# A graph kernel's edge messages: rows spread by three bf16 products instead of one in fp32

## The chip, the cores and the metric

The kernel runs on one core of a Trainium2 chip. The metric is the device time of one execution in microseconds (us). The core has five engines that run their own instruction streams and wait for each other by semaphores: TensorE (PE; its weight loads are shown as PEld), VectorE (DVE), ScalarE (ACT), GpSimd (POOL) and SyncE (SP, which only issues DMAs here). Sixteen DMA engines serve all queues.

## The reference, cut to what matters

Two graph layers on 32768 nodes of width 256 and 524288 edges that are sorted by target. Layer 0 is attention within blocks of 128 nodes; layer 1 passes messages along the edges in both directions:

```python
h = jnp.maximum(_layernorm(x, axis=-1), 0.0)
x = x + _L0_gnn_ref(h, ...)                      # attention in blocks of 128 nodes
h = jnp.maximum(_layernorm(x, axis=-1), 0.0)     # "h1" in the kernel
# layer 1, _L1_gnn_ref (h is batch-normalised first)
a_in = jax.ops.segment_sum(feat_in[src] * iw[:, None], dst, num_segments=N)
a_out = jax.ops.segment_sum(feat_out[dst] * ow[:, None], src, num_segments=N)
# then gates (sigmoid, tanh) on a_in, a_out and h
```

The change concerns `a_out`: each edge takes the row of its target node `dst`, times a weight, and adds it to the row of its source node `src`. The kernel does the weight matrices afterwards, so what is moved along the edges is `h1` itself, in fp32.

## The kernel before

Work comes in this order: sorting and tables (to about 1000 us), then the stage that the change touches (to about 9000 us), then adding up the messages by target and by source (to about 15100 us), then the gates.

In the touched stage two things are woven together by hand.

*Attention groups.* `group(g)` handles 512 nodes (four blocks of 128). It does not emit code but fills `todo`, a list of functions by step: `@at(t)` puts one at step t. A block b has its attention at steps from B = 17 + 11 b: scores (`sc`), their maxima (`nm`, VectorE), exponentials (`pr`, ScalarE), their transposes (`pt`, TensorE) and the copy of these (`PT`), the products with the values, `o`, the output product `y`, then `x1g` (VectorE) and its row statistics. At b = 2 (B = 39) and b = 3 (B = 50) the second layer norm follows: `std` at B + 17, `nmr` on VectorE at B + 18, the row `h1g` on ScalarE at B + 18 + n, its transpose on TensorE at B + 19 + n (into `pt` for block 1, into `sc` for the others; each of these has one buffer), its copy `h1T` on ScalarE at B + 20 + n. Blocks 0 to 2 are done together at b = 2 (n = 0 to 2, steps 57 to 61), block 3 at b = 3 (steps 68 to 70). `x1_d`, `h1_d` and `h1T_d` are the results' copies in DRAM. `h1_d` is read twice: by the spreading described next, and by the later stage that adds up by target.

*Spreading.* `spread(k, lo, hi)` takes a third of the edges (k = 0, 1, 2) in items of 128 edges whose targets lie in one block of 128 nodes. `turns` runs 64 items to a turn, 4352 items in 68 turns, and mostly four turns to a loop round. The first 63 turns each carry one attention group: the group's step u is emitted at step 64 r + u of turn r, behind the items' own work. An item i passes through `steps` at fixed distances: `fetch` (SP loads the 128 rows of the target block as `hb`, 10 buffers) at t = i, `spread_lanes` at i + 4, `select` at i + 6 (`selT`, four items at a time: a 0/1 matrix of which row each edge takes; and `oh`, which source block each edge goes to), `rank` (three bf16 products into `R`), `product` (`mp` = `selT` times `hb`, two buffers) and `place` (`jk`, on VectorE) at i + 8, `scale` (ScalarE writes `mp` times the edge's weight to `msg`) and `scatter` (POOL sends the messages to their places in `msg_d`) at i + 9. So at step t TensorE ranks and multiplies item t - 8. All engines but POOL run in the order written here:

```python
steps = ((0, fetch), (4, spread_lanes), (6, select), (8, rank), (8, product), (8, place), (9, scale), (9, scatter))
```

In each step the items' parts are emitted first, then `for f in todo.get(t, ()): f()`, the group's functions in the order in which `group` put them there: those of an earlier block ahead of those of a later one.

Of the kernel before, what the change touches and what calls it, by code (L numbers as in the profile page):

```python
# [11 lines left out]
F32 = mybir.dt.float32  # L12
# [7 lines left out]
P = 128  # L20
H = 8
DH = 32
D = H * DH
KC = D // P
HC = H // KC
GB = 4
# [122 lines left out]
BF16 = mybir.dt.bfloat16  # L149
NB = 256  # L150
T1 = 128
# [348 lines left out]
def gnn_kernel(ctx, tc, x, src, dst, edge_attr, edge_type, w_in_e, w_out_e,  # L500
               Wq, bq, Wk, bk, Wv, bv, Wo, bo, gate_table, We, be,
               gamma, beta, W_in, b_in, W_out, b_out, W_x2i, b_x2i, W_h2h, out):
    nc = tc.nc
    N = x.shape[0]
# [4 lines left out]
    dram = ctx.enter_context(tc.tile_pool(name="dram", bufs=1, space=DRAM))  # L509
# [33 lines left out]
    x1_d = dram.tile([N, D], F32, name="x1_d")  # L543
    h1T_d = dram.tile([D, N], F32, name="h1T_d")
    h1_d = dram.tile([N, D], F32, name="h1_d")
    rec_d = dram.tile([E + T2, 4], F32, name="rec_d")
    ends = [sum(PH[:k + 1]) for k in range(len(PH))]
    assert ends[-1] == E
# [11 lines left out]

    x1_g = x1_d.rearrange("(g b p) d -> g p b d", b=GB, p=P)
    h1_g = h1_d.rearrange("(g b p) d -> g p b d", b=GB, p=P)
    h1T_g = h1T_d.rearrange("(c p) (g n) -> g p c n", p=P, n=GN)


# [15 lines left out]
    for k, (lo, hi) in enumerate(edges):  # L581
# [5 lines left out]
        at = lambda t, f: t[rs, f, 0:CS]  # L587
        of = lambda f, i: tabr_d[rs, i:i + CT, f].rearrange("c (a i) -> c a i", i=4)[:, :, 1:4]
        _, _, r = item_tables(tc, cpool, cn, f"o{k}", scnt[k], 0, T3, CS, 1, NCO[k], hi - lo, [
            ("first", of(0, 0)), ("to", of(1, LAG)),  # L590
            ("keep", at(tabb_d, 1)), ("node", at(tabb_d, 2))])
# [20 lines left out]
    def numbers(ap, most):  # L612


        return [v.with_bounds(max_val=m) for v, m in zip(nc.values_load_multi_w_load_instructions(
            ap, engines=(mybir.EngineType.SP,), min_val=0, max_val=int(OUT),
            skip_runtime_bounds_check_because="bounded in item_tables")[1], most)]
# [21 lines left out]
    with tc.tile_pool(name="ld", bufs=1) as lp:  # L639
# [4 lines left out]
        for k in range(K):  # L644
            n, node = NC1[k], itp[k][1]
# [15 lines left out]
        g = lp.tile([P, 1], F32, name="g")  # L661
        nc.vector.tensor_copy(g, lead)
        for k in range(K):
            left = lp.tile([P, 1], F32, name="left")
            nc.vector.tensor_scalar(left, g, -1.0, float(NG), op0=ALU.mult, op1=ALU.add)
            at = lambda i: slice(i * K + k, i * K + k + 1)
# [20 lines left out]
    with ExitStack() as c1:  # L687

        ap = c1.enter_context(tc.tile_pool(name="a_1", bufs=1))
# [23 lines left out]
        xg, xb, x1g, h1g = (ap.tile([P, GB, D], F32, name=n) for n in ("xg", "xb", "x1g", "h1g"))  # L713
        hT, qT, h1T = (ap.tile([P, KC, GN], F32, name=n) for n in ("hT", "qT", "h1T"))
        nmr = ap.tile([P, GB], F32, name="nmr")

        mv, rstd = ([ap.tile([P, GB] + w, F32, name=f"{n}{i}") for i in range(2)] for n, w in (("mv", [2]), ("rstd", [])))

        def group(g, bias=None):
# [3 lines left out]
            def at(t):  # L723
                def put(f):
                    todo.setdefault(t, []).append(f)
                return put
# [9 lines left out]
            def transposed(name, rows):  # L736
                tp = a_ps.tile([P, KC, P], F32, name=name)
                for k in range(KC):
                    nc.tensor.transpose(tp[:, k], rows[:, k * P:(k + 1) * P], ident)
                return tp  # L740

            @at(0)
            def _():
                nc.scalar.dma_start(xg, x_g[g])
# [82 lines left out]
            for b in range(GB):  # L827
                B = 17 + 11 * b
                cols = slice(b * P, (b + 1) * P)
                s = {}  # L830
# [86 lines left out]
                for n, u in enumerate(range(bs.start, bs.stop)):  # L917
                    h = {}

                    @at(B + 18 + n)  # L920
                    def _(u=u):
                        nc.scalar.activation(h1g[:, u], x1g[:, u], AF.Relu, bias=nmr[:, u:u + 1], scale=rstd[1][:, u:u + 1])

                    @at(B + 19 + n)
                    def _(u=u, h=h):
                        h["tp"] = transposed("pt" if u == 1 else "sc", h1g[:, u])

                    @at(B + 20 + n)
                    def _(u=u, h=h):
                        nc.scalar.copy(h1T[:, :, u * P:(u + 1) * P], h["tp"])  # L930
# [4 lines left out]

            @at(B + 19)
            def _():
                nc.sync.dma_start(h1_g[g], h1g)

            @at(B + 21)  # L940
            def _():
# [8 lines left out]
        def alone(g, bias=None):  # L950
            todo = group(g, bias)
            for t in sorted(todo):
                for f in todo[t]:
                    f()
# [12 lines left out]
        sp = c1.enter_context(tc.tile_pool(name="p_s", bufs=2))  # L967
        op = c1.enter_context(tc.tile_pool(name="p_o", bufs=8))
        ip = c1.enter_context(tc.tile_pool(name="p_i", bufs=NM))
        hp = c1.enter_context(tc.tile_pool(name="p_h", bufs=10))  # L970
# [21 lines left out]
        def spread(k, lo, hi):  # L992
# [61 lines left out]
            def fetch(i, q, c, turn):  # L1054
                if q % 4 == 0:
                    c["at"] = numbers(c["row"][:, q:q + 4], [N - P] * 4)
                hb = turn["hb", i] = hp.tile([P, D], F32, name="hb")
                nc.sync.dma_start(hb, h1_d[ds(c["at"][q % 4], P)])

            def spread_lanes(i, q, c, turn):  # L1060
                if q % 4 == 0:
# [3 lines left out]

            def select(i, q, c, turn):
                if q % 4 == 0:
                    sel = turn["sel", i // 4] = sp.tile([P, 4, T1], F32, name="selT")
                    nc.vector.tensor_scalar(sel, turn["bc"], cn["lane"], None, op0=ALU.is_equal)
                oh = turn["oh", i] = op.tile([P, NB], BF16, name="oh")  # L1070
                nc.vector.tensor_scalar(oh, cn["iota1"], c["ed"][:, 0, q:q + 1], None, op0=ALU.is_equal)  # L1071

            def product(i, q, c, turn):
                mp = turn["mp", i] = pp.tile([P, D], F32, name="mp")
                nc.tensor.matmul(mp, turn["sel", i // 4][:, q % 4], turn.pop(("hb", i)), start=True, stop=True)  # L1075

            def add(what, of, to, turn):
                oh = turn["oh", of]
# [34 lines left out]


            steps = ((0, fetch), (4, spread_lanes), (6, select), (8, rank), (8, product), (8, place), (9, scale), (9, scatter))

            def turns(begin_at, end, nr, groups):

                with tc.For_i(begin_at, end, nr, hint_engines=ENGINES) as it:
                    cs, turn, todo, n = [], {}, {}, nr * CI  # L1120
                    last = steps[-1][0]
                    with tc.manual_schedule(engines=IN_ORDER):
                        for t in range(n + last):
                            r, q = divmod(t, CI)
                            if r < nr:
                                after = ds((it + (r + 1)).with_bounds(min_val=0, max_val=NC1[k]), 1)
                                if q == 0:
                                    cs.append({})
                                    begin(cs[r])
                                    if groups is not None:  # L1130
                                        for u, fs in group((it + groups + r).with_bounds(min_val=0, max_val=NG - 1)).items():
                                            assert u < CI + last
                                            todo.setdefault(t + u, []).extend(fs)
                                if q == 10:
                                    window(after)
                                if q == 24:
                                    more = derive(after)
                                if q >= 24:
                                    next(more, None)
                            for lag, step in steps:  # L1140
                                i = t - lag
                                if 0 <= i < n:
                                    step(i, i % CI, cs[i // CI], turn)
                            for f in todo.get(t, ()):
                                f()
                        add("ones_b", n - 1, n, turn)
                        add("triu", n - 2, n, turn)
                        add("triu", n - 1, n - 1, turn)
# [41 lines left out]
    with ExitStack() as c2:  # L1190
        fp = c2.enter_context(tc.tile_pool(name="q_f", bufs=1))
        wp = c2.enter_context(tc.tile_pool(name="q_w", bufs=2))
        sp = c2.enter_context(tc.tile_pool(name="q_s", bufs=4))
        mp = c2.enter_context(tc.tile_pool(name="q_m", bufs=8))
# [144 lines left out]
    with ExitStack() as c3:  # L1339
# [10 lines left out]
        with tc.For_i(0, NG // UE, 1) as it:  # L1350
            for u in range(UE):
                g = it * UE + u
# [71 lines left out]
```

## Time and profile before

| | |
|---|---|
| median of 12 runs | 17246.58 us (17218.29 to 17273.27) |
| the profiled execution | 17258.26 us, its span 17256.5 us |
| granted TensorE clock, mean | 0.913 |
| TensorE busy | 14052.0 us (81%) |
| VectorE, ScalarE, POOL busy | 58%, 39%, 54% |
| products `mp` (line L1075) | 8704 matmul instructions, two to a product |
| DMA | 2975.49 MB, 172 GB/s over the span |

In the profile a line such as L1075 is that line of the kernel file. `out<-in` names the tiles, with numbers left out of the names: `h_d` stands for `h1_d`, `x_d` for `x1_d`, `msg_d` for each of the three. A matmul's duration reaches from its start to its modelled end, and matmuls overlap; so the pace of TensorE is read from one start to the next. "[1.90 <-ACT pr L851]" behind a line of the timeline is the engine's idle time ahead of it and who ended it. A table of waits gives, for each pair of waiter and releaser, total us, times and longest. In the table by stretches the last columns are the granted clock of TensorE (1 is full speed), the DMA engines' busy share and GB/s.

### The profile page before, as it was taken

How to read it: one execution, taken by the hardware profiler on the slowest of the kernel's cores; microseconds unless marked ns; L12 is line 12 of the kernel's file. 1: busy time of each engine (PE TensorE's matmuls, PEld its weight loads, DVE VectorE, ACT ScalarE, POOL GpSimd, SP SyncE). 2: the span in 40 equal slices, each digit the busy share in tenths (PEclk: the TensorE clock that was granted, in tenths of full speed). 3: DMA queues.
4: the chain of work that ended last, by engine and by line, in shares of the span. 5: the costliest groups of instructions: out<-in, count | busy, mean ns of one | idle time of the engine just before them, and what ended most of it. 6: DMA issues, size and time to landing. Idle time of an engine off the chain costs nothing. (4 is left out here: it accounts for less than half of the span.)

```text
span 17256.5 us, 292322 instructions
## 1 busy us (share of the span) xinstructions
PE 14052.0 (81%) x71746; PEld 10243.3 (59%) x71746; DVE 10066.7 (58%) x33799; ACT 6724.1 (39%) x16865; POOL 9321.8 (54%) x9307
## 2 busy tenths in 40 slices
PE   2068888878888878888759999898888888888989
PEld 1045555555555555565547777777777777643433
DVE  8766667666766766776655555555555555422222
ACT  0034444444544444454434444444444444300000
POOL 0045555555555555555567777776767667622221
PEclk6589999989999989999879999999999999999999
DMA  1035555544554545555448888788878888843332
GB/s 64 10 119 165 165 165 164 161 150 159 168 163 159 164 127 163 167 165 162 155 155 243 243 241 243 233 240 231 236 227 237 228 236 240 197 129 106 110 117 91
DMA packets 1829630, 2975.49 MB, mean 172 GB/s; under 512 B 299498, under 2 KB 1288135, under 8 KB 1827670
## 3 DMA queue, kind: packets, MB, share of 16 engines
q1 hardware_dynamic: 1169398, 1550.90, 29.8%
q0 software_dynamic: 430768, 1160.40, 22.6%
q10 hardware_dynamic: 227888, 246.51, 4.6%
q8 instruction: 582, 9.54, 0.2%
q14 instruction: 994, 8.14, 0.2%
HBM read 2123.63 MB, written 1248.64 MB: 195 GB/s over the span
## 5 line engine op out<-in xcount | busy, mean ns | idle before, releaser
L1108 POOL DMA_INDIRECT msg_d<-msg,pi x4352 | 4298.2, 988 | 3027.8 <-ACT msg L1091 1087.7
L1230 POOL DMA_INDIRECT rows<-h_d,ixc x3584 | 3414.8, 953 | 1376.9 <-PE ps_i L1244 354.8
L1099 DVE SCALAR_TENSOR_TENSOR jk<-iota,edc,R 128x256 f32<-128x256 bf16 x4352 | 2076.4, 477 | 1914.2 <-PE R L1079 1882.4
L1091 ACT ACTIVATE msg<-mp,edc 128x256 f32<-128x256 f32 x4352 | 2064.1, 479 | 2749.5 <-PE mp L1075 2728.5
L1265 ACT ACTIVATE selo<-lane_row,sl 128x128 f32<-128x128 f32 x5040 | 1671.1, 393 | 3389.2 <-DVE sl L1262 2742.1
L1244 PE MATMUL ps_i<-rows,sel 128*128 128x257 f32 x8960 | 2504.3, 398 | 335.7 <-DVE acc L1248 259.1
L1075 PE MATMUL mp<-hb,selT 128*128 128x256 f32 x8704 | 2766.2, 401 | 8.0 <-ACT msg L1091 7.4
L1272 PE MATMUL ps_o<-m,selo 128*128 128x257 f32 x10080 | 2567.7, 392 | 216.9 <-ACT selo L1266 214.5
L1272 PEld LDWEIGHTS ps_o<-m,selo 128*128 128x128 f32 x10080 | 1868.2, 195 | 527.0 <-ACT selo L1266 166.7
L1244 PEld LDWEIGHTS ps_i<-rows,sel 128*128 128x128 f32 x8960 | 1564.8, 198 | 589.5 <-DVE acc L1248 370.6
L1237 DVE TENSOR_SCALAR sel<-lane_row,ed 128x128 f32<-128x128 f32 x4480 | 1395.4, 360 | 605.4 <-PE idle L1245 548.5
L1075 PEld LDWEIGHTS mp<-hb,selT 128*128 128x128 f32 x8704 | 1402.5, 203 | 82.9 <-ACT msg L1091 13.5
L1071 DVE TENSOR_SCALAR oh<-iota,edc 128x256 bf16<-128x256 bf16 x4352 | 1419.9, 326 | 4.1
L1079 PE MATMUL R<-oh,ones_b 128*128 128x256 bf16 x4352 | 1247.6, 287 | 119.3 <-DVE jk L1099 110.9
L1276 DVE SCALAR_TENSOR_TENSOR acc<-acc,blk,ps_o 128x257 f32<-128x257 f32 x1680 | 807.7, 481 | 835.3 <-PE ps_o L1272 700.0
L1079 PE MATMUL R<-oh,tri 128*128 128x256 bf16 x4352 | 1239.8, 285 | 0.0
L1079 PE MATMUL R<-oh,triu 128*128 128x256 bf16 x4352 | 1233.2, 284 | 0.0
L1248 DVE SCALAR_TENSOR_TENSOR acc<-acc,blk,ps_i 128x257 f32<-128x257 f32 x2240 | 1073.2, 479 | 213.9 <-DMA sin_d<-acc 97.9
L1262 DVE TENSOR_SCALAR sl<-m,blk 128x3 f32<-128x3 f32 x1680 | 426.2, 254 | 1131.9 <-DMA m<-msg_d 1117.9
L1230 POOL DMA_INDIRECT rows<-h_d,ixh x896 | 854.8, 954 | 374.8 <-issue 138.6
L1266 ACT ACTIVATE selo<-selo,one 128x384 f32<-128x384 f32 x1680 | 1035.1, 616 | 52.5
L1245 PE MATMUL idle<-lane_row,sel 128*128 128x128 f32 x4480 | 850.0, 278 | 138.0 <-DVE sel L1237 121.5
(366 smaller groups left out, 20255.4 us busy)
## 6 DMA issues: line engine op xcount, KB each, us to landing
m<-msg_d SPq DMA_DIRECT2D x1680, 396.0 KB
hb<-h_d SPq DMA_DIRECT2D x4352, 128.0 KB
sin_d<-acc SPq DMA_DIRECT2D x2240, 128.5 KB
sout_d<-acc SPq DMA_DIRECT2D x1680, 128.5 KB
msg_d<-msg,pi POOLq DMA_INDIRECT x4352
more<-sout_d ACTq DMA_DIRECT2D x128, 514.0 KB
rows<-h_d,ixc POOLq DMA_INDIRECT x3584
a<-sin_d ACTq DMA_DIRECT2D x64, 514.0 KB
```

The source lines that it names most:

```text
L1071: nc.vector.tensor_scalar(oh, cn["iota1"], c["ed"][:, 0, q:q + 1], None, op0=ALU.is_equal)
L1075: nc.tensor.matmul(mp, turn["sel", i // 4][:, q % 4], turn.pop(("hb", i)), start=True, stop=True)
L1079: nc.tensor.matmul(R[to % 2], cn[what], oh, start=False, stop=False, skip_group_check=True)
L1091: nc.scalar.activation(msg[:, q % 4, 0:D], turn.pop(("mp", i)), AF.Copy, scale=c["ed"][:, 1, q:q + 1])
L1099: nc.vector.scalar_tensor_tensor(jk, cn["iota1"], c["ed"][:, 0, q:q + 1], R[i % 2], op0=ALU.is_equal, op1=ALU.mult, accum_out=c["pf"][:, q ...
L1108: s = nc.gpsimd.indirect_dma_start(out=msg_d[k][:], out_offset=bass.IndirectOffsetOnAxis(ap=c["pi"][:, j:j + 1], axis=0), in_=msgs[i // 4 ...
L1230: nc.gpsimd.indirect_dma_start(out=rows[(2 * i + r) % NR][:, 0:D], out_offset=None, in_=h1_d[:], in_offset=bass.IndirectOffsetOnAxis(ap=(i ...
L1237: nc.vector.tensor_scalar(sel[:, r], cn["lane_row"], c["ed"][:, 0, r, i:i + 1], c["ed"][:, 1, r, i:i + 1], op0=ALU.is_equal, op1=ALU.mult)
L1244: nc.tensor.matmul(ps, sel[:, r], rows[(2 * i + r) % NR], start=(r == 0), stop=(r == 1))
L1248: nc.vector.scalar_tensor_tensor(acc[0][i % NA], acc[0][(i - 1) % NA], c["blk"][:, 0, i:i + 1], c.pop(("t_ps", i)), op0=ALU.mult, op1=ALU.add)
L1265: nc.scalar.activation(sel[:, r], cn["lane_row"], AF.Abs, bias=sl[:, r:r + 1])
L1272: nc.tensor.matmul(ps, sel[:, r], m[:, r, 0:FW], start=(r == 0), stop=(r == T3 // P - 1))
```

## The change

The rows of `h1` are also stored as three bf16 parts, whose sum is the fp32 row: the first is `h1g` rounded to bf16, the second is what is left of it, rounded, the third the rest of that. ScalarE makes the first two, VectorE takes the differences and writes the third, four blocks a group, at steps B + 19 to B + 21 (+ n). The parts go to a new DRAM tensor `h1s_d` by a DMA on SP at step B + 22; the store of `h1_d` moves from SP's queue to ScalarE's. `fetch` loads the three parts (192 KB an item in place of 128 KB), `selT` becomes bf16, and `product` multiplies it with each part in turn and adds the three up in `mp`. All else stays.

```diff
+    h1s_d = dram.tile([N, 3, D], BF16, name="h1s_d")
+    h1s_g = h1s_d.rearrange("(g b p) s d -> g p b s d", b=GB, p=P)
...
+        h1s = ap.tile([P, GB, 3, D], BF16, name="h1s")
+        rest = ap.tile([P, GB, D], F32, name="rest")
...
                     @at(B + 19 + n)
                     def _(u=u, h=h):
                         h["tp"] = transposed("pt" if u == 1 else "sc", h1g[:, u])
 
+                    @at(B + 19 + n)
+                    def _(u=u):
+                        nc.scalar.copy(h1s[:, u, 0], h1g[:, u])
+
+                    @at(B + 20 + n)
+                    def _(u=u):
+                        nc.vector.tensor_sub(rest[:, u], h1g[:, u], h1s[:, u, 0])
+                        nc.scalar.copy(h1s[:, u, 1], rest[:, u])
+
+                    @at(B + 21 + n)
+                    def _(u=u):
+                        nc.vector.tensor_sub(h1s[:, u, 2], rest[:, u], h1s[:, u, 1])
+
                     @at(B + 20 + n)
                     def _(u=u, h=h):
                         nc.scalar.copy(h1T[:, :, u * P:(u + 1) * P], h["tp"])
...
             @at(B + 19)
             def _():
-                nc.sync.dma_start(h1_g[g], h1g)
+                nc.scalar.dma_start(h1_g[g], h1g)
+
+            @at(B + 22)
+            def _():
+                nc.sync.dma_start(h1s_g[g], h1s)
...
-                hb = turn["hb", i] = hp.tile([P, D], F32, name="hb")
-                nc.sync.dma_start(hb, h1_d[ds(c["at"][q % 4], P)])
+                hb = turn["hb", i] = hp.tile([P, 3, D], BF16, name="hb")
+                nc.sync.dma_start(hb, h1s_d[ds(c["at"][q % 4], P)])
...
-                    sel = turn["sel", i // 4] = sp.tile([P, 4, T1], F32, name="selT")
+                    sel = turn["sel", i // 4] = sp.tile([P, 4, T1], BF16, name="selT")
...
-                nc.tensor.matmul(mp, turn["sel", i // 4][:, q % 4], turn.pop(("hb", i)), start=True, stop=True)
+                hb = turn.pop(("hb", i))
+                for part in range(3):
+                    nc.tensor.matmul(mp, turn["sel", i // 4][:, q % 4], hb[:, part], start=(part == 0), stop=(part == 2))
```

## The prediction

> **What bounds the kernel now.** I read the page's first two parts, then the table by stretches of time, the waits of the stage that the change touches, and last the timeline of one turn of that stage.
>
> ```profile
> span 17256.5 us, 292322 instructions
> PE 14052.0 (81%) x71746; PEld 10243.3 (59%) x71746; DVE 10066.7 (58%) x33799; ACT 6724.1 (39%) x16865; POOL 9321.8 (54%) x9307
> 1127.00:8391.00 7264.00, 6069.34 (x34963) 4261.94 (x34962) 5010.94 (x18308) 3542.22 (x9109) 4069.49 (x4040) 0.91 0.50 160
> 8520.00:8910.00 390.00, 240.77 (x1561) 170.91 (x1560) 229.23 (x973) 129.60 (x328) 256.95 (x260) 0.80 0.53 172
> ```
>
> The two stretches (PE, PEld, DVE, ACT, POOL busy, then TensorE's clock, DMA share, GB/s) are the spreading stage: 63 turns of 64 items that carry a group of attention along, some 115 us each, and the last turns without a group, 97 us each. With a group PE is the busiest engine (84%), without one it is at 62%, and POOL's row is 0.99 us busy plus 0.30 idle an item, 64 x 1.29 = 83 of the 97 us. So a saving on PE counts in the 63 turns alone. There PE has these waits:
>
> ```profile
> PE pt L857 <- ACT pr L851: 194.1, 114, 1.9
> PE mm L739 <- DVE xn L770: 142.2, 41, 9.2
> PE pt L857 <- ACT F L1038: 134.1, 57, 2.4
> PE sc L739 <- ACT h1g L922: 93.4, 57, 4.8
> ```
>
> Each (total us, times, longest) ends at an attention step: PE waits once a turn for ScalarE or VectorE at fixed places. I number the steps of a turn as the code does (step t ranks and multiplies item t-8). Reading the trace step by step, PE's waits lie at steps 35 (2.4 us), 46 (1.5), 57 (1.9), 68 and 69 (2.3), 72 (0.4 to 0.9), and short ones at 17, 30, 31, 41, 58, 63. Between them PE is dense:
>
> ```profile
> 4063.01 0.27 PE L1079 MATMUL R<-oh,triu 128*128 128x256 bf16 x1
> 4063.12 0.27 PE L1079 MATMUL R<-oh,tri 128*128 128x256 bf16 x1
> 4063.23 0.60 PE L1075 MATMUL mp<-hb,selT 128*128 128x256 f32 x2
> 4063.67 0.27 PE L1079 MATMUL R<-oh,ones_b 128*128 128x256 bf16 x1
> ```
>
> Starts are what counts, not durations: a bf16 product of 256 columns follows the last one after 0.11 us, each with a weight load of its own, and the fp32 product holds PE for 0.44 us.
>
> **The product.** Three bf16 products take 3 x 0.11 = 0.33 us in place of 0.44: 0.11 us less for each of 4352 items, 479 us if all of it counted. In a turn it counts only where no later wait swallows it. A wait swallows the saving of every step since the work began that it waits for: at 35 the chain starts with `jk` of step 33 (three steps lost), likewise 46 and 57 (three each), 68/69 (VectorE is busy from step 66 on: four), 72 (two), 17, 31 and 58 (two each), 30, 41 and 63 (one each). That is 24 of 64 lost, 40 x 0.11 = 4.4 us kept a turn. In the last turns, nothing.
>
> The selection in bf16 keeps its input, 512 fp32 elements from PSUM (0.74 us a call); I cost it at nothing either way (bounds: the same, or half of 0.74 us for every fourth item, on VectorE, which is not what PE waits for in the dense steps).
>
> **The fetches.** `hb` grows from 128 to 192 KB an item. Queue 1 moved 1550.9 MB in 1169398 packets with 29.8% of 16 engines, 70 ns for 1.33 KB; 512 bytes more are at most 27 ns, x 128 packets / 16 = 0.22 us of 1.75 us: DMA share 0.50 to 0.62. PE waits for `hb` hardly at all today, and a fetch goes out eight steps (13 us) ahead: cost nothing. The store of the parts is 768 KB and sits on SP at step 72, after VectorE's last part of step 71; queued behind it are SP's fetches 73 and later, which read that tensor and so wait for its landing. Today they wait for the 512 KB store: 114.3 us in 40 times, 2.9 us each; 1.5 times that is 4.3 us, inside the 13 us. If the cover is gone it is 4.3 x 63 = 270 us. The old store moves to ACT's queue: an issue there takes 0.38 us (row of `x_d`), on ACT at step 69, where it waits for the `h1g` that ACT itself has just made; `xn` and not ACT is late there, so nothing; bounds 0 and 0.38 x 63 = 24 us.
>
> **The splitting.** Per group four row blocks, each with two ACT copies and two VectorE subtractions of 128x256. Nearest rows: ACT's `h1g` (SBUF to SBUF, 0.49 us to the next start) and the `h1T` copy (from PSUM, 0.25); I take 0.5, the SBUF row. VectorE's 128x256 addition is 0.42 us; I take 0.4 (0.33 to 0.42). That is 4 us of ACT and 3.2 us of VectorE a turn, little beside their idle time, but the place decides. Blocks 0 to 2 are split at steps 58 to 62, where ACT has this to do:
>
> ```profile
> 4080.05 0.49 ACT L1091 ACTIVATE msg<-mp,edc 128x256 f32<-128x256 f32 x1
> 4080.41 0.62 ACT L922 ACTIVATE h1g<-x1g,nmr,rstd 128x256 f32<-128x256 f32 x1
> 4080.90 0.50 ACT L1091 ACTIVATE msg<-mp,edc 128x256 f32<-128x256 f32 x1
> 4081.26 0.40 ACT L930 COPY h1T<-sc 128x256 f32<-128x256 f32 x1
> 4081.51 0.65 ACT L922 ACTIVATE h1g<-x1g,nmr,rstd 128x256 f32<-128x256 f32 x1
> 4082.02 0.62 ACT L863 COPY PT<-pt 128x512 f32<-128x512 f32 x1
> ...
> 4081.76 0.48 DVE L1099 SCALAR_TENSOR_TENSOR jk<-iota,edc,R 128x256 f32<-128x256 bf16 x1 [1.61 <-PE R L1079]
> ...
> 4082.69 0.69 PE L739 MATMUL pt<-ident,h1g 128*128 128x128 f32 x2
> ```
>
> ACT has no gap here, and PE's transposition at 4082.69 waits for the `PT` copy, which frees `pt`. Into this row go, ahead of `PT`: the first copy of block 0 (0.5), the second copy of block 0 (0.5) and the first of block 1 (0.5). The second copy waits for VectorE's subtraction, emitted in the same step, which is in line behind `jk` of step 59 (4081.76) and `pi`: it runs from 4082.44 to 4082.84, so ACT stands until 4082.9, then 0.5 + 0.25 (`h1T`) + 0.5 + 0.5 (`h1g`) + 0.6 (`PT`) gives 4085.3: PE is 2.6 us later. In a turn at full clock `jk` comes some 0.5 us earlier, and it is 1.9. Bounds: 0.75 (three copies at 0.25, no waiting) to 2.9. I take **2.2 us**. ACT's own messages wait behind it, and POOL's scatters behind those; POOL has 30% to spare.
>
> Steps 60 to 63: two further subtractions and copies a step; ACT's message copy of step 62 comes late for PE's product of step 63 (two `mp` buffers), and `o` behind the subtractions: 0 to 1.0, I take **0.6**. Steps 70 and 71 (block 3): two subtractions of 0.4 ahead of the `xn` that PE already waits for at step 72: **0.8** (0.4 to 1.2).
>
> **The clock.** The granted clock is 1 or 0.5:
>
> ```profile
> 3930.00:3940.00 10.00, 10.00 (x40) 7.43 (x41) 2.19 (x9) 0.95 (x2) 6.19 (x7) 0.50 0.30 108
> 3950.00:3960.00 10.00, 10.00 (x73) 7.69 (x71) 7.74 (x32) 4.58 (x14) 5.50 (x6) 1.00 0.53 168
> ```
>
> It changes at multiples of 3.41 us. I counted over the windows of 3.41 us at full clock in this stage how much of each matmuls stream, transpositions left out: below 0.3, 146 of 147 are followed by half clock; between 0.3 and 0.4, 12 of 103; above, none of 1441. The new wait at step 59 leaves PE idle for 3.1 us (with transpositions 3.3). A window falls below 0.3 if it overlaps that by 2.4 us: (3.3 + 3.41 - 4.8)/3.41 = 0.57 of the alignments, and then 3.41 us at half clock lose 1.7: 1.0 us. The four older waits each grow by the 0.3 us that they swallow: 0.3/3.41 = 0.09 more drops each, of some 3.5 us (mostly two windows): 1.3 us. Together **2.3 us**, bounds 0 and 3.5.
>
> The Trainium skill ("TensorE: Matmul & The Clock Gate", the practical table) says that only a PE-idle gap of more than about 3 us brings half clock back, and Part 4 that transpositions do not count as busy. The second agrees with the count above; the first is too mild for this trace, where the clock falls after waits of 1.9 us. By the page's rule the clock's term would be near zero, the sum -0.8 us a turn, and the time 17,200.
>
> **Sum.** A turn: -4.4 + 2.2 + 0.6 + 0.8 + 2.3 = +1.5 us; x 63 = +95 us. The profiled execution took 17258.3 us (span 17256.5, 1.8 around it), 11.7 over the median of 17246.6; with +95 it would be 17,353, and the median 17,340.
>
> **The rivals.**
> Faster: the splitting fits into slack. ACT is busy 49% of the stage, and if copies cost 0.25 and the subtraction is not late, the turn is -4.4 + 0.75 + 0.4 = -3.2 us, -200 us, 17,045. It speaks for it that 4 us of work is small; against it that ACT's row above has no gap. It decides when PE's wait before `pt<-ident,h1g` grows by less than 1.5 us and the clock keeps its 0.91. Chance 0.30.
> A draw: saving and waits cancel within 34 us (0.2%, about what a measurement of this kernel can tell from no change), 17,250. Chance 0.12.
> Clock worse: PE streams a quarter less in each product, and two more windows a turn go to half clock: 2 x 1.7 x 63 = 214 us more, 17,550. Against it: products in dense steps stay dense. Chance 0.10.
> The change does not do what it says: each bf16 product pays its full row duration (0.287) instead of its pace, 0.86 for 0.44 us: 0.42 x 40 x 63 = 1060 us more, 18,300. The rank products' pace speaks against it. Or `hb` arrives late, +270. Together 0.05.
> The forecast itself, slower by 35 to 200 us: 0.43.
>
> **Range.** Lowest terms: -4.4 + 0.75 + 0 + 0.4 + 0 = -3.2 (17,045). Highest: 2.9 + 1.0 + 1.2 + 3.5 - 3.8 (a saving kept in 35 steps only) = +4.8, +300 (17,550). So 17,040 to 17,560. Faster by over 0.2%: 0.30; within: 0.12; slower: 0.43 + 0.10 + 0.05 = 0.58.
>
> **What would show it.** Right: three `mp` products 0.11 us apart; a PE wait of some 3 us at `pt<-ident,h1g` for `PT`, and ACT idle before its second `h1s` copy, released by `rest`; the wait for `xn` longer; the clock of the stage under 0.91. Wrong: group turns shorter than 112 us, ACT's copies at 0.3 us, no wait at step 59; or PE waiting for `hb`.

## The result and the profile after

| | before | after |
|---|---|---|
| median | 17246.49 us (30 runs) | 17498.29 us (7 runs, 17482.53 to 17511.78) |
| ratio after / before | | 1.0147, 95% interval 1.0138 to 1.0157 |
| end of the touched stage in the profiled execution | 8969 us | 9215 us |

Slower by 252 us: the forecast's side, inside its range, and 2.6 times its +95. The stage that the change touches ends 246 us later, so there is nothing to look for elsewhere. The page of the changed kernel, its first lines and the row of granted clock, then the same stretch of the stage as in the prediction (length, busy time of PE, PEld, DVE, ACT and POOL, clock, DMA share, GB/s):

```profile
span 17501.5 us, 298145 instructions
PE 13960.1 (80%) x76098; PEld 10283.7 (59%) x76098; DVE 10165.0 (58%) x34311; ACT 6864.3 (39%) x17377; POOL 9335.5 (53%) x9307
PEclk6578888888888888888879999999999999999999
L1099 PE MATMUL mp<-hb,selT 128*128 128x256 bf16 x13056 | 2378.1, 296 | 12.1 <-DMA hb<-h1s_d 7.7
```

```profile
1127.00:8391.00 7264.00, 5832.91 (x37720) 4183.54 (x37719) 4966.55 (x18250) 3568.83 (x9317) 3962.56 (x3917) 0.86 0.61 196
```

PE's busy time falls, and the kernel is slower: busy time is no measure here. Two numbers of the stretch moved as forecast (the DMA share, 0.50 to 0.61 where 0.62 was worked out; PE waits 7.7 us for `hb` in the whole stage), and one moved far more than forecast: the clock, 0.91 to 0.86. PE's longest waits between 1500 and 8300 us (total us, times, longest), without the row of 18 waits between the loop's rounds:

```profile
PE mm L743 <- DVE xn L774: 160.8, 56, 8.9
PE pt L861 <- ACT F L1060: 146.9, 55, 2.7
PE pt L743 <- ACT PT L867: 141.7, 55, 2.8
```

The third is the new one. Before, the same pair waits 3 times in all:

```profile
PE pt L739 <- ACT PT L863: 3.1, 3, 1.0
```

Now it waits once a turn, 2.6 us each. It is the wait at step 59 that the prediction placed, and the timeline of a turn shows the row that causes it as it was worked out (start, duration, then what; in brackets the idle time before it and who ended it):

```profile
3829.49 0.43 ACT L935 CAST h1s<-h1g 128x256 bf16<-128x256 f32 x1
...
3830.94 0.42 DVE L939 TENSOR_TENSOR rest<-h1g,h1s 128x256 f32<-128x256 f32 x1
...
3831.39 0.41 ACT L940 CAST h1s<-rest 128x256 bf16<-128x256 f32 x1 [0.61 <-DVE rest L939]
3831.71 0.37 ACT L948 COPY h1T<-sc 128x256 f32<-128x256 f32 x1
3831.97 0.41 ACT L935 CAST h1s<-h1g 128x256 bf16<-128x256 f32 x1
3832.28 0.60 ACT L926 ACTIVATE h1g<-x1g,nmr,rstd 128x256 f32<-128x256 f32 x1
3832.78 0.57 ACT L867 COPY PT<-pt 128x512 f32<-128x512 f32 x1
...
3833.41 0.45 PE L743 MATMUL pt<-ident,h1g 128*128 128x128 f32 x2 [2.78 <-ACT PT L867]
...
3834.94 0.85 PE L1099 MATMUL mp<-hb,selT 128*128 128x256 bf16 x3
...
3836.01 0.48 PE L877 MATMUL mm<-vg,PT 128*128 128x33 f32 x2
```

ScalarE stands 0.61 us for VectorE's difference, and the three new copies stand ahead of `PT`. A copy holds ScalarE for about 0.31 us (3831.97 to 3832.28), where 0.5 was taken. What follows was not in the forecast: the three products at 3834.94 take 0.85 us; an item earlier, at 3830.14, they took 0.49. The same turn by stretches: steps 57 and 58, step 59, steps 60 to 63, steps 64 to 67 (columns as above):

```profile
3824.88:3830.03 5.15, 2.56 (x21) 1.76 (x18) 4.30 (x17) 5.11 (x13) 3.94 (x4) 1.00 0.59 183
3830.03:3834.73 4.70, 1.92 (x15) 1.12 (x13) 1.18 (x5) 3.09 (x8) 0.30 (x1) 0.89 0.34 108
3834.73:3844.25 9.52, 9.52 (x49) 7.70 (x48) 6.09 (x24) 3.78 (x11) 3.83 (x5) 0.52 0.31 98
3844.25:3848.17 3.92, 3.92 (x34) 3.17 (x32) 3.36 (x12) 2.12 (x5) 3.01 (x4) 1.00 0.70 225
```

PE has no gap in the third stretch and runs at half speed through nearly all of it. The wait of 2.8 us costs itself, and behind it half clock takes some 4.6 of the next 9.52 us.

### The profile page after: what moved, and what is told of

Same layout as the page of the kernel before. It is cut to its first block, busy times and chain, and to the rows that moved or that the text cites. A ratio compares the mean times of both kernels' runs of the same rounds, so it can differ in the third digit from the quotient of the medians.

```text
span 17501.5 us, 298145 instructions
## 1 busy us (share of the span) xinstructions
PE 13960.1 (80%) x76098; PEld 10283.7 (59%) x76098; DVE 10165.0 (58%) x34311; ACT 6864.3 (39%) x17377; POOL 9335.5 (53%) x9307
## 3 DMA queue, kind: packets, MB, share of 16 engines
q0 software_dynamic: 430768, 1160.40, 22.1%
## 5 line engine op out<-in xcount | busy, mean ns | idle before, releaser
L1099 PE MATMUL mp<-hb,selT 128*128 128x256 bf16 x13056 | 2378.1, 296 | 12.1 <-DMA hb<-h1s_d 7.7
L1099 PEld LDWEIGHTS <-selT 128*128 128x128 bf16 x13056 | 1388.4, 106 | 280.3 <-issue 13.3
L1103 PE MATMUL R<-oh,ones_b 128*128 128x256 bf16 x4352 | 1294.1, 297 | 155.0 <-DVE jk L1123 144.4
L1093 DVE TENSOR_SCALAR oh<-iota,edc 128x256 bf16<-128x256 bf16 x4352 | 1358.8, 312 | 4.1
L1103 PE MATMUL R<-oh,tri 128*128 128x256 bf16 x4352 | 1294.5, 297 | 0.0
L1103 PE MATMUL R<-oh,triu 128*128 128x256 bf16 x4352 | 1290.3, 296 | 2.6
```

Of the source, the lines that this page charges most:

```text
L1099: nc.tensor.matmul(mp, turn["sel", i // 4][:, q % 4], hb[:, part], start=(part == 0), stop=(part == 2))
L1103: nc.tensor.matmul(R[to % 2], cn[what], oh, start=False, stop=False, skip_group_check=True)
```

## The experiments

Theory A (the forecast's mechanism, with a larger clock term): the splitting makes PE wait at step 59, the wait takes the clock away, and the half clock is most of the loss. Rivals: B, the work itself (copies and differences) costs the time, whatever the clock; C, the larger fetches hold PE or VectorE back; D, the loss comes from where the split stands in the turn, so that another place gives the saving back.

The chip matters for reading the numbers. The second group of runs went to one on which the kernel before took 17507.0 us, and the changed kernel some 240 us more than above too; its stage ends at the same time as above, so these extra us lie outside it. The kernel before has no profile from that chip; its row below is from the first one. On the chips of the other groups every kernel, the one before included, takes some 2000 us more (before: 19435 to 19537 us); those come last.

Per turn, over turns 4 to 59 of each kernel's trace, I split the time into PE's idle time, what half clock took from its busy time, and the remainder, PE's work as at full clock (us; the split is good to about 0.7, because not all of PE's work doubles at half clock: eight value products of 33 columns take 0.81 us at full clock and 1.56 at half):

| kernel | work | idle | lost to half clock | turn |
|---|---|---|---|---|
| before | 92.5 | 19.0 | 6.9 | 118.5 |
| after (`changed_again`) | 85.8 | 24.1 | 12.6 | 122.4 |
| `products_alone_2` | 86.0 | 22.1 | 9.8 | 117.8 |
| `keep_clock_2` | 88.5 | 23.0 | 7.1 | 118.6 |
| `late_split_2` | 86.5 | 24.9 | 9.4 | 120.8 |

**The changed kernel again**, unedited, so that the others have a neighbour on their chip.

> The changed kernel as it is, as the yardstick of this chip. If the chip's kernel before takes 17,246 us, this takes 17,498 (ratio 1.0147). On the chip of the last four runs, where the kernel before took 19,435 us and engines stood at 'issue' in every stage, theory 'wait and clock' gives the same 250 us as an addition, 19,690.

17738.3 us against 17507.0, ratio 1.012 (1.0103 to 1.0137), the stage's end at 9215 us as before. The difference after minus before is 3.95 us a turn, x 63 = 249 us.

**The products without the splitting.** The parts are stored as they lie; fetches, stores and products stay.

```diff
-        def group(g, bias=None):
+        def group(g, bias=None, split=True):
...
-                    @at(B + 19 + n) ... (the four functions' copies and differences)
+                    if split: ...
...
-   group((it + groups + r)...)
+   group((it + groups + r)..., split=False)
```

> No splitting in the turns (left out, so that old parts are stored and the output is not the reference's); products, fetches and store as changed. Theory 'wait and clock': 63 x 3.4 to 63 x 4.4 us less than the kernel before, ratio 0.984 to 0.988. Rival 'data': 1.010 to 1.015.

17414.07 us, 0.9938 (0.9921 to 0.9954): 93 us faster than before (1.5 us a turn), less than half of what was expected of it. Against rival C this decides: full fetches, and faster. The profiled execution was the slowest of its four, 49 us above their median, so the table's 0.7 us a turn is below the 1.5 of the medians, and what the trace gives for this kernel may be off by as much. In that trace, of the 6.6 us of work saved in a turn, 3.1 turn into idle time and 2.8 are given back to the clock. PE waits at the same steps as before, at most of them 0.2 to 0.5 us longer. The row of step 35 (total us, times, longest) comes to 2.7 us a time, where the 134.1 us in 57 times of before are 2.35:

```profile
PE pt L861 <- ACT F L1061: 155.0, 58, 2.7
...
PE pt L861 <- ACT pr L855: 107.8, 59, 2.1
```

What that does to the clock is clearest at step 46 (the second row): 1.50 us before, after which the clock never fell, 1.82 us now, after which steps 46 to 49 lose 0.58 us a turn to half clock.

**The wait filled.** The changed kernel, with the three products of one item in step 59 repeated six times into the same `mp` (the first of each three starts it anew). 18 products of 0.109 us, 2.0 us, stand where PE would wait. Nothing else differs; the copies, differences and fetches are all there.

```diff
+        FILL = {59: 6}
...
-                for part in range(3):
-                    nc.tensor.matmul(mp, ..., start=(part == 0), stop=(part == 2))
+                for _ in range(1 + c["more"].get(q + 8, 0)):
+                    for part in range(3):
+                        nc.tensor.matmul(mp, ..., start=(part == 0), stop=(part == 2))
...
+                                    cs[r]["more"] = FILL if groups is not None else {}
```

> Products of item 51 repeated six times in step 59, ahead of the wait for PT. Theory 'wait and clock': 5 us a turn less than the changed kernel, ratio to the kernel before 0.996 to 1.000. If the clock is not what costs: 1.0147 or more.

17498.95 us, 0.9997 (0.9987 to 1.0006): 239 us faster than the changed kernel, with 2 us a turn more for PE to do. The timeline of a turn at step 59, PE alone, then the stretches of step 59 and of steps 60 to 63:

```profile
3735.29 2.63 PE L1101 MATMUL mp<-hb,selT 128*128 128x256 bf16 x21
3738.60 0.44 PE L743 MATMUL pt<-ident,h1g 128*128 128x128 f32 x2 [0.68 <-ACT PT L867]
```

```profile
3735.08:3739.53 4.45, 3.77 (x31) 2.86 (x30) 1.19 (x5) 2.43 (x7) 0.00 (x0) 0.94 0.26 70
3739.53:3745.91 6.38, 5.48 (x51) 4.56 (x49) 5.67 (x23) 3.70 (x11) 3.96 (x4) 1.00 0.51 161
```

ScalarE is about as late as without the fill (step 59 takes 4.45 us here and took 4.70), and steps 60 to 63 take 6.38 us at clock 1.00 instead of 9.52 at 0.52. Over all turns steps 59 to 63 fall from 14.54 to 10.81 us, 3.73 of the 3.82 us by which a turn is shorter. Rival B is refuted: the work is the same. On this chip the change costs 231 us (17738.3 less 17507.0), and filling one wait takes 239 away; what brought them was the clock, since half clock takes 0.5 us of steps 59 to 63 here and took 5.7.

**The splitting four steps later**, blocks 0 to 2, behind the step where `PT` is wanted.

```diff
+                late = 4 if b < GB - 1 else 0
...
-                    @at(B + 19 + n)
+                    @at(B + 19 + n + late)
```
(and the same for the functions at B + 20 + n and B + 21 + n)

> Splitting of blocks 0 to 2 four steps later, on a chip without the stalls at 'issue' if this is one. Theory 'wait and clock': 470 us less than the changed kernel, 17,030 to 17,150, ratio to the kernel before 0.988 to 0.995. Rivals 'plain work' and 'data': as the changed kernel, ratio 1.012 to 1.015.

17627.49 us, 1.0064 (1.0042 to 1.0085): 111 us better than the changed kernel, still slower than before, a miss. Steps 59 to 63 go down as wanted, 14.54 to 8.67 us. Then steps 64 to 67 take 1.6 us more and 68 to 71 2.1 us more, and half clock at the older waits comes back too (0.9 us more at steps 20 to 22 and 35 to 41). The waits table has two rows for it:

```profile
PE R L1104 <- DVE jk L1124: 235.4, 56, 7.4
...
PE mm L899 <- ACT oT L893: 58.8, 56, 1.3
```

Both can be followed in the timeline of one turn:

```profile
3776.08 0.40 ACT L941 CAST h1s<-rest 128x256 bf16<-128x256 f32 x1 [1.01 <-DVE rest L940]
...
3777.11 1.13 PE L899 MATMUL mm<-wo,oT 128*128 128x256 f32 x4 [1.29 <-ACT oT L893]
...
3782.83 0.43 DVE L734 BATCH_NORM_STATS2 st<-xg 128x6 f32<-128x256 f32 x1 [2.38 <-DMA xg<-in_x]
3782.97 2.33 POOL L752 TENSOR_TENSOR xb<-xg,bo_b 128x1024 f32<-128x1024 f32 x1 [3.49 <-DMA xg<-in_x]
...
3783.91 1.47 DVE L1094 TENSOR_SCALAR oh<-iota,edc 128x256 bf16<-128x256 bf16 x1
3785.31 0.47 DVE L1124 SCALAR_TENSOR_TENSOR jk<-iota,edc,R 128x256 f32<-128x256 bf16 x1
...
3785.84 0.37 PE L1104 MATMUL R<-oh,ones_b 128*128 128x256 bf16 x1 [5.20 <-DVE jk L1124]
```

The copy of a part, itself late by 1.01 us for `rest`, now stands ahead of `oT`. And at step 68 the engines arrive early: VectorE waits 2.38 us for the next group's `xg`, and its `oh`, 0.28 us elsewhere, takes 1.47 beside POOL's addition. Rival D is half right (the place is what costs), but the next place has waiters too, and here time won ahead of a DMA was given back to it.

**On the other chips.** There the same program carries further waits. The first take of the filled wait ran on such a chip:

> The changed kernel, and in step 59 of each turn with a group the three products of item 51 are repeated six times, ahead of the wait for PT: some 2 us of the wait are filled with matmuls, nothing else changes. Theory 'wait and clock': the wait for PT ends when it ended before, but full clock stays through steps 60 to 63: 5 us a turn less, 17,498 - 315 = about 17,180 to 17,250. If the wait alone costs, or the work of the other engines: no change, 17,498, or up to 63 x 0.5 = 30 us more. Rival 'data': 17,498.

19648.31 us, 1.0106 (1.0081 to 1.0131). The changed kernel itself has no run on such a chip, so what the fill gains there is not known; half clock takes 0.9 us of steps 59 to 63, against 3.0 in the splitting alone on the same chip (below). Three rows of its table of waits, and then the only one of the three that stands in the table of `keep_clock_2`, the same program ("issue" is idle time with no releaser in the profile):

```profile
PE R L1106 <- issue: 154.2, 75, 3.6
DVE jk L1126 <- issue: 151.7, 142, 4.5
POOL msg_d L1135 <- issue: 1350.0, 2073, 10.1
```

```profile
POOL msg_d L1135 <- issue: 837.1, 1613, 3.0
```

At fixed steps (13, 17, 33, 34, 52, 63) PE is idle for 0.8 to 2.5 us a turn longer than on the other chip (`products_alone` against `products_alone_2`). In single turns it can be seen that PE, VectorE and ScalarE stand and are released together, without a releaser that the profile names. In one turn of `split_alone` at step 34:

```profile
4084.38 0.60 PE L1097 MATMUL mp<-hb,selT 128*128 128x256 f32 x2
...
4087.84 0.48 DVE L1121 SCALAR_TENSOR_TENSOR jk<-iota,edc,R 128x256 f32<-128x256 bf16 x1 [3.50 <-remote]
4087.87 0.33 SPq L1080 DMA_DIRECT2D hb<-h_d  x1
4087.88 0.47 ACT L1113 ACTIVATE msg<-mp,edc 128x256 f32<-128x256 f32 x1 [3.77 <-remote]
```

PE's products are done, and three engines that wait for them start some 3 us late at one time. What causes it is not settled. These waits bring half clock of their own (0.8 us at step 17 with the products alone, none on the other chip), so sizes from these chips are not set against the sums above; what a kernel does at one step can still be read.

The splitting alone (spreading back to the fp32 product and `h1_d`, the split and its store kept):

```diff
-                hb = turn["hb", i] = hp.tile([P, 3, D], BF16, name="hb")
-                nc.sync.dma_start(hb, h1s_d[...])
+                hb = turn["hb", i] = hp.tile([P, D], F32, name="hb")
+                nc.sync.dma_start(hb, h1_d[...])
```
(`selT` back to F32, one product)

> The changed kernel with the spreading put back: one fp32 product from the fp32 rows; the splitting and the store of the parts stay (the parts are read by nobody). Theory 'wait and clock' (the splitting delays the PT copy at step 59, PE idles 2.6 us there, and half clock follows through steps 59 to 63, 5.7 us a turn): the wait and the low clock stay and the products' saving of about 4 us a turn is gone: 17,498 + 63 x 4 = about 17,750, granted clock in the turns about 0.86. Rival 'data' (the larger fetches and the larger share of the DMA engines slow the stage): the fetches are small again, so near the kernel before, 17,250 to 17,330. Rival 'plain work' (4 us of ScalarE and VectorE a turn cost what they cost, wherever they are): about 17,246 + 63 x 4 = 17,500 with the clock near 0.91.

19671.51 against 19435.21 us, 1.011 (1.0081 to 1.0139); on another chip (`split_alone_2`) 1.0159 (1.0142 to 1.0176). That is 3.8 to 4.9 us a turn, about what the whole change costs, and a miss for theory A as it was put: 17,750 would be a ratio of 1.029. Two of its figures were too high: the products alone had saved 1.5 us a turn and not 4, and half clock takes 3.0 and 4.3 us of steps 59 to 63 in these two traces and not 5.7. By the time alone rival B's 17,500 fits as well; what speaks against B is the filled wait. Its table of waits has the row of step 59 at the same length as the changed kernel, so the splitting makes it and not the new products:

```profile
PE pt L743 <- ACT PT L867: 153.5, 57, 3.2
```

The first takes of two kernels from above:

> The changed kernel without the splitting in the turns: the copies and subtractions are left out there, so that the store writes old parts and the output is not the reference's; three bf16 products, fetches of 192 KB and the store stay. Theory 'wait and clock': the wait of step 59 and its half clock are gone, what stays is the saving of the prediction, 4.4 us a turn, less some drops of the clock after the older waits, 1 us: 17,246 - 63 x 3.4 to 63 x 4.4 = 16,970 to 17,030. Rival 'data': slower than the kernel before by most of the 252 us, 17,400 to 17,500. Rival 'plain work': 16,970, as the first.

> The changed kernel with the splitting of blocks 0 to 2 four steps later (steps 62 to 66 instead of 58 to 62, behind the PT copy); all work stays. Theory 'wait and clock': wait (1.9 us) and half clock (5.7 us) of step 59 vanish, 7.5 us a turn, 17,498 - 470 = about 17,030, faster than the kernel before; 17,030 to 17,150 if the later place brings short waits. Rival 'plain work' and rival 'data': the same work and the same bytes, so 17,450 to 17,500.

Both are misses. The products alone took 1.0039 (1.0026 to 1.0053), slower than the kernel before where the other chip had 0.9938; what the further waits do to their saving was not separated. The late splitting took 1.0098 (1.0073 to 1.0123).

Then I tried to keep ScalarE's row in order: the split's functions are gathered and put last in their steps, so that `PT` is ahead of them.

```diff
+            behind = []
+            def after(t): ...          # puts (t, f) into behind
...
-                    @at(B + 19 + n)
+                    @after(B + 19 + n)
...
+            for t, f in behind:
+                at(t)(f)
```
(and the same for the functions at B + 20 + n and B + 21 + n)

> The changed kernel with the same splitting in the same steps, but emitted behind the other functions of each step, so that at step 59 the PT copy comes ahead of the part copies on ScalarE. Theory 'wait and clock': the wait of step 59 and its half clock are gone, and what the products alone gave stays: a turn of 117.8 to 118.5 us against 118.5 of the kernel before, ratio to the kernel before 0.994 to 1.000. Rival 'plain work': the same work in the same steps, as the changed kernel, 1.012 to 1.0147.

19581.08 against 19444.39 us, 1.0066 (1.0046 to 1.0087); twice more 1.0127 (1.011 to 1.0144) and 1.0075 (1.0058 to 1.0091): a miss. The long wait is gone, 0.56 us each instead of 2.7:

```profile
PE pt L750 <- ACT PT L874: 32.2, 57, 1.4
```

The half clock is not: steps 59 to 63 still lose 4.1 us a turn to it (1.7 with the products alone on such a chip), and the trace has the clock down already in step 58, behind waits of 0.9, 0.4 and 2.5 us in steps 52, 56 and 57; the thin steps 60 and 61 then follow. The order alone was not enough here; that other waits take the clock is read from the trace and not tried by itself. So the waits were filled as well, with repeated products, in three kernels: the reordered one, the changed one and the one before.

```diff
order_and_fill:    FILL = {20: 5, 35: 6, 46: 4, 57: 5, 68: 4}
changed_and_fill:  FILL = {20: 5, 35: 6, 46: 4, 57: 5, 59: 6, 68: 4}
before_and_fill:   FILL = {35: 4, 57: 4, 68: 3}        # fp32 products
```

> The kernel of order_only, and the products of one item are repeated 5, 6, 4, 5 and 4 times at steps 20, 35, 46, 57 and 68, ahead of the long waits there. If half clock behind the older waits eats the products' saving (the products alone saved 3.8 us a turn at full clock and lost 3.2 to it): a turn of 112 to 114 us, ratio 0.977 to 0.985. If not, as order_only.

> The changed kernel with repeated products at steps 20, 35, 46, 57, 59 and 68 (5, 6, 4, 5, 6, 4 times). Theory 'wait and clock': of 13 us at half clock a turn outside the loop's end some 10 go, which is 5 to 8 us of time: a turn of 115 to 117 us, ratio 0.985 to 0.995. Otherwise no better than the 0.9997 with step 59 alone.

> The kernel before with its fp32 products repeated 4, 4 and 3 times at steps 35, 57 and 68. It loses 6 us a turn at half clock outside the loop's end: 3 to 4 us a turn less, ratio 0.985 to 0.990. If the fill lengthens the waits that it stands in: 1.00 or more.

| kernel | ratio to before, same chip |
|---|---|
| `order_and_fill` | 1.004 (1.0026 to 1.0054); 1.0143 (1.0126 to 1.016); 1.0041 (1.0026 to 1.0055) |
| `changed_and_fill` | 1.0086 (1.0065 to 1.0108) |
| `before_and_fill` | 0.9933 (0.9917 to 0.995); 0.9991 (0.998 to 1.0002) |

Filling does cut the clock's loss (16.4 us a turn in `order_only`, 10.9 in `order_and_fill`), but the turn only goes from 134.5 to 134.0 us: PE's work grows by 8.6 us, and its idle time falls by only some 3.5 (at step 59 it grows again, from 0.6 to 1.8). All three kernels fell short of the gain that was expected of them. No version of the changed kernel beat the one before on these chips. Whether `order_and_fill` would on a chip like the second group's stays open, since none of its runs fell on one. The kernel before gains from a fill by 0.7% on one chip and by nothing that can be told on another.

## Why the prediction was right in sign and wrong in size

Term by term, us a turn, with what the table above gives:

| term | forecast | measured | from |
|---|---|---|---|
| saving kept | -4.4 | -3.5 | `products_alone_2` - before: work -6.6, idle +3.1 |
| (a) step 59, wait for `PT` | +2.2 | +2.1 | idle in step 59: 0.46 without the split, 2.56 with it |
| (b) step 63 | +0.6 | -0.2 | idle in step 63: 0.21, then none |
| (c) step 72, `xn` | +0.8 | +0.6 | idle in step 72: 0.28, then 0.88 |
| clock, older waits | +1.3 | +2.8 | `products_alone_2` - before, 6.9 to 9.8 |
| clock, splitting | +1.0 | +2.9 | after - `products_alone_2`, 9.8 to 12.6 |
| given back at steps 68 and 69 | | -0.6 | idle there 4.03, then 3.41 |
| sum | +1.5 | +3.95 | x 63: 95, 249 us |

(The measured rows add up to 4.1; the difference to 3.95 is within what the split into work, idle time and clock is good for. Between the two rows of the clock some 0.8 us can be shifted, since the profiled execution of `products_alone_2` was slow by that much; their sum does not rest on it.)

**What held.** The path of the loss, ScalarE's row without a gap, and its price: 2.1 for 2.2. Two errors in its working cancel: the copies hold ScalarE for 0.31 us instead of 0.5, and PE gets to the point earlier than I let it, its products being shorter, so its wait is longer than its delay. (Copies at 0.3 us stood among the signs of being wrong; they came, and the wait came all the same.) The pace of the bf16 products: 6.6 to 6.8 of the 7.0 us of work are gone. The fetches cost nothing: SP waits 134.7 us in 38 times for the new store, 3.5 us each (4.3 forecast), and PE does not feel it. The count of waits that swallow the saving was nearly right, 3.1 us against 24 x 0.11 = 2.6.

**The step that failed** is the clock's term, 2.3 forecast, 5.7 measured, and it is the whole miss: without it the turn would be 1.7 us shorter than before (0.8 forecast). Two things in it were wrong.

First, the new wait. I took a drop in 57% of the turns and one window of 3.41 us at half clock, 1.0 us. The clock falls in every turn, and half clock then holds for 12.5 us of steps 59 to 63 on the average (1.3 before). Steps 59 to 63 lose 5.7 us to it (0.7 before, 1.55 with the products alone); 1.3 us come back at other steps, which gives the net 2.9. I had asked what makes the clock fall, and not what brings it back. Counting again over the windows of 3.41 us of both traces (before and after), now those at half clock and with transpositions counted: of 388 windows in which matmuls streamed less than 0.65 of the time, none was followed by full clock; of 264 above 0.85, all were. Over half of steps 60 and 61 goes to value products of 33 columns (twice eight, 1.56 us each time) and a transposition (0.43 us); steps 60 to 63 are 49 matmul instructions in 9.52 us, with PE never idle and PEld busy for 7.70. PE is full there and streams little. Of all windows at half clock, 160 had PE busy for over 98% of the time and streamed less than 0.70, and none of them was followed by full clock; 245 were as busy and streamed above 0.85, and all were. So the half clock outlives the wait: it lasts for three windows in 31 of the 56 turns and for five in the other 25. `keep_clock_2` shows the size of the effect; that thin products are what keeps the clock low rests on the count and was not tried by itself.

The rule of the Trainium skill that was weighed ("TensorE: Matmul & The Clock Gate", the table in "Why this matters for your kernels": no gaps of more than about 3 us, or half clock comes back) would have given 17,200 by the estimate above. The clock fell here behind waits of 1.8 us (step 46) and of 2.6 (step 59), so it is further off than the forecast. The same page (Part 1) says that some 3.4 us of sustained busy time bring full clock back. Here PE was busy without a gap for 9.5 us at 0.52, so having no gap is not enough.

Second, the older waits. I took 0.3/3.41 = 0.09 more drops at each. The waits did grow by 0.2 to 0.3 us, but a drop is not a matter of chance alignment alone: step 46 went from none to one that costs 0.58 us a turn, steps 20 to 22 from nothing to 0.7, steps 35 to 41 from 2.6 to 3.3, and steps 59 to 63 lose 0.9 more behind the wait of step 57. A likely reason, argued and not tried by itself: a cheaper product leaves less streaming between two waits, so windows fall that had just held.

**The rivals.** "Fits into slack" is ruled out by the 2.6 us wait; "clock worse" had the mechanism (two more windows a turn, 17,550) at 0.10 and came nearest, 52 us off, though for another reason than it gave: the windows are lost behind a wait, where products are already thin, and not in dense steps. "Does not do what it says" and the late `hb` are ruled out by the pace and by 7.7 us of waiting.

## What to carry to other kernels

A saving on PE between two waits makes both waits longer and the stretch thinner, so price it with the clock: of 6.6 us saved a turn here, 3.1 went into longer waits, 2.8 into half clock, and 0.7 were left in the profiled execution (1.5 by the medians). For a new wait on PE, look at what runs in the windows behind it: here narrow products ran there, and the low clock stayed for three windows or five. Two cures were tried where chips could be compared. Moving the helper's work four steps later gave back 111 of the 231 us and met new waiters. Filling the wait with products that change nothing gave back 239 us for 2 us of extra work a turn, which makes the changed kernel as fast as the one before and no faster.

## What was not expected of the hardware

- Half clock lasted through 9.5 us of PE work without a gap, over half of its first two steps being 33-column products. In the counts of these traces fuller windows were needed to leave half clock (none under 0.65 of the time streaming, all above 0.85) than to keep full clock (above 0.4, transpositions left out).
- The same program ran some 2000 us longer on some chips, with further waits at fixed steps (in one of them VectorE and ScalarE start some 3 us after the products were done); the cause is open.
- A `tensor_scalar` of 0.28 us took 1.47 us beside POOL's 2.33 us addition; in `late_split_2` that is the median of the 42 of its kind that overlap such an addition, and 0.28 that of the 4918 others.
